# Reordering the first attention layer of a two-layer cross-attention kernel: scores, projection, maxima and a small sum change places

## Chip, cores and metric

The kernel runs on one core of one Trainium2 chip, in one launch. The metric is the device time in microseconds (us); a lower one is better. A profile, where one is shown, is of one execution. Engines are named as in the profile: PE is TensorE (matmuls and transposes), PEld its weight loads, DVE is VectorE, ACT is ScalarE, POOL is GpSimd, SP is SyncE, which here only issues transfers.

## What is computed

There are 32 samples, each with 256 tokens of 256 features, of `x` and of a context. All is in fp32. Two layers follow each other; the reference, cut to what matters:

```python
def L0(tgt, memory, Wq, Wk, Wv):          # 16 heads of 16 features
    q, k, v = heads(tgt @ Wq.T), heads(memory @ Wk.T), heads(memory @ Wv.T)
    probs = softmax(einsum('bhqd,bhkd->bhqk', q, k) / sqrt(16))
    att = merge(einsum('bhqk,bhkd->bhqd', probs, v))
    return tgt + att[0]                    # sample 0's attention is added to every sample

def L1(ctx, x):
    norm_X, norm_F = layernorm(ctx, n1w, n1b), layernorm(x, n2w, n2b)
    attended = softmax(norm_F @ norm_X.T / sqrt(256)) @ norm_X
    h = gelu(attended @ fc1_w.T + fc1_b)   # 4 hidden features
    cross = h @ fc2_w.T + fc2_b
    norm_c = layernorm(cross, n3w, n3b)
    self_att = softmax(norm_c @ norm_c.T / sqrt(256)) @ norm_c
    return norm_F + g2 * (cross + g1 * self_att)

x = L0(x, ctx); x = L1(ctx, x)
```

Only `att[0]` is used, so layer 0 (L0) needs the attention of sample 0 alone. Its result, `att`, is added to each sample of `x`; after that every sample goes through layer 1.

## The kernel before

**L0.** The 16 heads are worked in four "fours", j = 0 to 3. For each four the same steps follow each other, on different engines:

- `head_queries(j)`: PE computes four heads' scores with a row for each query (tiles `sq`, one PSUM bank for a head), eight matmuls of 32 rows (`pair_products`, L445).
- `head_maxima(j, sq, heads)`: DVE takes each query's largest score, negated, into `m_all` (L486), one instruction for a head.
- `head_less(j)`: PE transposes these maxima (`pm`, L493), and DVE adds them to the queries (`qmT`, L498), so that the next scores come out with the maximum already taken off. What it returns is the DVE step; `head_less(j)()` does both at once.
- `head_keys(j)`: PE computes the scores again, with a row for each key (tiles `sk`), and ACT takes their exponentials (`eT_h`, L507), one instruction for a head.
- `head_values(j, copy, by_pairs)`: PE sums exponentials times values (`ph`, L357, eight matmuls), and `copy` brings the result out of PSUM (`col_h`, L368), on ACT or DVE. With `by_pairs` the first two heads' matmuls stand ahead of the others'.
- `head_turned(j)`: PE transposes that (`pt_h`, L375). What it returns, called `weighted`, is DVE's division and its write into `att` (L527, L528).

Between these steps stands work for layer 1: statistics of the context (`stats(n)`, DVE, two instructions L211 for a sample), their moments for four samples (`moments_c` on POOL, L222 to L236, of which L227 is a power; `moments_ahead` on DVE but for the power), the context's normalization (`even_normed` on POOL, L316; `odd_normed` on ACT, L322), and the preparation of small constants (`setup_bias`: PE sums `b1f` into `p_b1f`, L579, and DVE adds a row to make `fc1b_all`, L582; `setup_outer`, `setup_gram`). `project_values(1)` makes the second half of the values `v1` (`pp_v`, L430; copied by ACT, L437).

**After L0.** DVE adds `att` to the first samples (`add_first`, L828) and takes their statistics; POOL makes `rs_x` from them (L227, `first_moments`). For later samples POOL issues transfers that add `att` in memory, four samples each (`add_attention`, L751). Layer 1 then runs one sample a step (`first_step`): normalized `x` is transposed (`turn_x`), scores (`cross_scores`, L779), softmax, transposes and sums. The second attention, over six features, and the output follow in an order written out by hand.

**What sets the order.** Nothing is rescheduled: `tc.manual_schedule()` keeps every engine's instructions in the order in which the program text issues them. An instruction waits, with all behind it on its engine, for the semaphores of those it depends on. [...] The scores rotate over six of them (`four_banks`: `h0` to `h3` and two called `et`). The two others have the tag `tp` and are shared by `pp_v`, `pm`, `ph`, `pt_h`, `p_b1f` and the transposes: the next such tile takes the bank of an earlier one, and its first matmul waits until that one's last reader is done.

Of the kernel before, what the change touches and what calls it, by code (L numbers as in the profile page):

```python
# [22 lines left out]
QB = 4  # L23
# [4 lines left out]
def tile_xattn_seq(  # L28
# [51 lines left out]
    def bank(tag, name):  # L80
        return ps.tile([P, NC, D], F32, tag=tag, name=name)
# [131 lines left out]
    def moments(st, n, name, eng=None):  # L213

        eng = eng or nc.gpsimd

        def t(what, c=1, bufs=2):
            return small.tile([P, n, c], F32, tag=f"{what}{n}", name=f"{what}_{name}", bufs=bufs)

        sm, df, sq, v4, ve, nm = t("sm", 2), t("df"), t("sq"), t("v4"), t("ve"), t("nmean")  # L220
        rs, nmr = t("rs", 1, 3), t("nmr", 1, 3)
        eng.tensor_sub(df, st[:, :, 1:2], st[:, :, 4:5])  # L222
        eng.tensor_add(sm, st[:, :, 1:3], st[:, :, 4:6])
        eng.tensor_mul(sq, df, df)
        eng.tensor_scalar(v4, sm[:, :, 1:2], 4.0 / D, 4 * EPS, ALU.mult, ALU.add)
        eng.tensor_add(ve, v4, sq)
        nc.gpsimd.tensor_tensor(  # L227
            rs.rearrange("p n o -> p (n o)"),
            ve.rearrange("p n o -> p (n o)"),
            neg_half[:, 0:n],  # L230
            ALU.pow,
        )

        def product():
            eng.tensor_scalar(nm, sm[:, :, 0:1], -0.5, 0.0, ALU.mult, ALU.add)
            eng.tensor_mul(nmr, nm, rs)  # L236

        if eng is nc.gpsimd:
            product()
            return rs, nmr  # L240
        return rs, nmr, product
# [11 lines left out]
    def stats_c(n):  # L253
        q, b = n // QB, n % QB
        statistics(st_tile(q - 1)[:, 0, b], cq_of[q][:, b])
# [5 lines left out]
    def flat(st):  # L261
        return st.rearrange("p b t c -> p (b t) c")

    def moments_c(q):
        rn = moments(flat(st_of[q - 1][:, 0]), TQ, f"c{q}")
        for b in range(QB):
            mc_of[q * QB + b] = *rn, b * NC
# [44 lines left out]
    def even_normed(*ns):  # L312
        for n in ns:
            rs, nmr, i = mc_of[n]
            row = cq_of[n // QB][:, n % QB, 0, :]
            nc.gpsimd.tensor_scalar(row, row, rs[:, i, :], nmr[:, i, :], ALU.mult, ALU.add)  # L316

    def odd_normed(*ns):
        for n in ns:
            rs, nmr, i = mc_of[n]  # L320
            row = cq_of[n // QB][:, n % QB, 1, :]
            nc.scalar.activation(  # L322
                row, row, AF.Identity, bias=nmr[:, i + 1, :], scale=rs[:, i + 1, :]
            )
# [22 lines left out]
    def by_columns(psum, name, weights, moving, copy=nc.vector.tensor_copy, by_pairs=False):  # L347
        return copy_columns(columns(psum, name, weights, moving, by_pairs), name, copy)
# [22 lines left out]
    def tokens_first(psum, src, name):  # L371

        pt = psum(f"pt_{name}")
        for t in range(NC):
            nc.tensor.transpose(pt[:, 0, t * P : (t + 1) * P], src[:, t * P : (t + 1) * P], ident)  # L375
        return pt[:, 0, :].rearrange("p (t b c) -> p t b c", t=NC, c=SL)
# [50 lines left out]
    def project_values(t, copy):  # L427
        pp = bank("tp", f"pp_v{t}")
        for dc in range(NC):
            nc.tensor.matmul(  # L430
                pp[:, t, :],
                c0T[:, dc, t * P : (t + 1) * P],
                wvT[:, dc, :],
                start=(dc == 0),
                stop=(dc == NC - 1),
            )
        copy(v1[:, t, :, 0:DK], pp[:, t, :].rearrange("p (h e) -> p h e", e=DK))  # L437

    def pair_products(*pairs):

        for t in range(NC):
            for p, lhs, rhs, dst in pairs:
                for i in range(2):
                    r = SL * (p % 2 * 2 + i)
                    nc.tensor.matmul(  # L445
                        dst[i][:, t, :],
                        lhs[r : r + SL, t * P : (t + 1) * P],
                        rhs[r : r + SL, :],
                        start=True,
                        stop=True,  # L450
                    )
# [4 lines left out]
    def four_banks(name):  # L456

        at = head_banks[0]
        head_banks[0] = (at + QB) % 6
        return [  # L460
            ps0.tile([P, NC, D], F32, tag=f"h{i}", name=f"{name}_{i}")
            if i < QB
            else bank("et", f"{name}_{i}")
            for i in ((at + n) % 6 for n in range(QB))
        ]
# [8 lines left out]
    def head_of(j, i):  # L474
        return 8 * (j // 2) + 2 * i + j % 2

    def head_queries(j):

        sq = four_banks(f"sq{j}")
        qk = qT[:, j, :], kT[:, j, :]  # L480
        pair_products((0, *qk, sq[0:2]), (1, *qk, sq[2:4]))
        return sq

    def head_maxima(j, sq, heads):
        for i in heads:
            nc.vector.tensor_reduce(  # L486
                m_all[:, j % 2, :, i, ones_at[j % 2]], sq[i], AX.X, ALU.max, negate=True
            )

    def head_less(j):  # L490
        pm = bank("tp", f"pm_{j}")
        for t in range(NC):
            nc.tensor.transpose(  # L493
                pm[:, 0, t * P : (t + 1) * P],
                m_all[:, j % 2, t].rearrange("p b c -> p (b c)"),
                ident,
            )
        return lambda: nc.vector.tensor_add(qmT[:, j % 2, :], pm[:, 0, :], qT[:, j, :])  # L498

    def head_keys(j):  # L500

        sk = four_banks(f"sk{j}")
        kq = kT[:, j, :], qmT[:, j % 2, :]
        pair_products((0, *kq, sk[0:2]), (1, *kq, sk[2:4]))
        eT_of[j] = wk.tile([P, QB, NC, D], F32, tag="eTq", name=f"eT_h{j}", bufs=2)
        for i in range(QB):
            nc.scalar.activation(eT_of[j][:, i], sk[i], AF.Exp)  # L507
# [4 lines left out]
    def head_values(j, copy=nc.scalar.copy, by_pairs=False):  # L512
        col_of[j] = by_columns(
            tp_bank,
            f"h{j}",
            lambda kt, i: v1[:, kt, head_of(j, i), :],
            eT_of.pop(j),
            copy,
            by_pairs,
        )  # L520

    def head_turned(j):
        pa = tokens_first(tp_bank, col_of.pop(j), f"h{j}")

        def weighted():
            rd = small.tile([P, NC, QB, 1], F32, tag="rdh", name=f"rd_h{j}")
            nc.vector.reciprocal(rd, pa[:, :, :, DK : DK + 1])  # L527
            nc.vector.tensor_mul(  # L528
                att.rearrange("p t (k i e d) -> p t k i e d", i=QB, e=2, d=DK)[
                    :, :, j // 2, :, j % 2, :  # L530
                ],
                pa[:, :, :, 0:DK],
                rd.to_broadcast([P, NC, QB, DK]),
            )

        return weighted
# [39 lines left out]
    def setup_bias():  # L576
        pb = bank("tp", "p_b1f")
        for dc in range(NC):
            nc.tensor.matmul(  # L579
                pb[:, 0, 0:FH], ones, b1f[:, dc, :], start=(dc == 0), stop=(dc == NC - 1)  # L580
            )
        nc.vector.tensor_add(fc1b_all, pb[:, 0, 0:FH], fc1b_bc)  # L582
# [78 lines left out]
    on_scalar = nc.scalar.copy  # L661

    by_vector = nc.vector.tensor_copy

    def stats(*ns):
        for n in ns:
            stats_c(n)
# [6 lines left out]
    sq = head_queries(0)  # L674
# [5 lines left out]
    sq = head_queries(1)  # L680
# [9 lines left out]
    head_less(1)()  # L690
    setup_outer()
    stats(3)
    project_values(1, on_scalar)
    moments_c(0)
    even_normed(0, 1, 2, 3)
    sq = head_queries(2)
    stats(4)
    head_maxima(2, sq, (0, 1))
    head_values(0)
    setup_bias()  # L700
    head_maxima(2, sq, (2, 3))
    head_keys(1)
    odd_normed(0, 1)
    weighted = head_turned(0)
    stats(5)
    head_less(2)()
    weighted()
    sq = head_queries(3)
    stats(6)
    head_maxima(3, sq, range(QB))  # L710
    head_values(1)
    odd_normed(2, 3)
    head_keys(2)
    weighted = head_turned(1)
    stats(7)
    moments_c(1)
    even_normed(4, 5)
    head_less(3)()
    weighted()
    head_keys(3)  # L720
    stats(8, 9, 10)
    head_values(2, by_vector)
    stats(11)
    odd_normed(4)
    head_values(3, on_scalar, True)
    c_ends = moments_ahead(2)
    weighted = head_turned(2), head_turned(3)
    for f in weighted:
# [632 lines left out]
```

## Time and profile before

| | |
|---|---|
| median of 3 runs | 230.23 us (229.31, 230.23, 233.49) |
| profiled execution | 233.63 us, of which the span from first to last instruction is 231.9 us |
| PE busy | 214.7 us, 93% of the span |
| DVE busy | 169.8 us, 73% |
| POOL busy | 174.8 us, 75% |
| ACT busy | 146.8 us, 63% |
| HBM | 17.73 MB read, 8.39 MB written |
| end of L0 (`att` complete) | 34.85 us from the span's start |

The page gives each engine's busy share, the chain of work that ended last (followed back from the last instruction, at each step to what released it), and groups of instructions by source line. A line of the timeline reads: start, duration, engine, source line, operation, output, input, shape, count, and in brackets how long the engine stood idle before it and what ended that. Times inside the span are counted from its start. The profiled execution is longer than the median; a sum made from its durations belongs to its own time.

### The profile page before, as it was taken

How to read it: one execution, taken by the hardware profiler on the slowest of the kernel's cores; microseconds unless marked ns; L12 is line 12 of the kernel's file. 1: busy time of each engine (PE TensorE's matmuls, PEld its weight loads, DVE VectorE, ACT ScalarE, POOL GpSimd, SP SyncE). 2: the span in 40 equal slices, each digit the busy share in tenths (PEclk: the TensorE clock that was granted, in tenths of full speed). 3: DMA queues.
4: the chain of work that ended last, by engine and by line, in shares of the span. 5: the costliest groups of instructions: out<-in, count | busy, mean ns of one | idle time of the engine just before them, and what ended most of it. 6: DMA issues, size and time to landing. Idle time of an engine off the chain costs nothing.

```text
span 231.9 us, 4950 instructions
## 1 busy us (share of the span) xinstructions
PE 214.7 (93%) x1797; PEld 155.8 (67%) x1797; DVE 169.8 (73%) x409; ACT 146.8 (63%) x299; POOL 174.8 (75%) x276
## 2 busy tenths in 40 slices
PE   7999898898999989999999999989989999999960
PEld 6766556576787768697897887866665666566540
DVE  1797989899988748667686686766384866588791
ACT  2544978698988285966789967456846753444410
POOL 6057598576989999999979999995189999993000
PEclk9999999999999999999999999999999995699996
DMA  6789997999959964180720000000000130444477
GB/s 212 271 310 371 394 383 148 194 256 236 207 104 335 275 117 170 34 151 2 133 51 1 3 0 0 3 4 4 4 0 3 51 133 0 181 184 181 185 281 264
DMA packets 18038, 33.81 MB, mean 146 GB/s; under 512 B 1175, under 2 KB 2142, under 8 KB 18014
## 3 DMA queue, kind: packets, MB, share of 16 engines
q1 hardware_dynamic: 12974, 24.33, 29.3%
q0 software_dynamic: 3696, 7.34, 18.1%
q10 hardware_dynamic: 1344, 1.84, 2.3%
q8 instruction: 14, 0.23, 0.4%
q14 instruction: 10, 0.08, 0.1%
HBM read 17.73 MB, written 8.39 MB: 113 GB/s over the span
## 4 chain that ended last, share of the span: by engine, by line
PE 53%; POOL 23%; DVE 14%; ACT 5%; issue 2%; DVEq 0%; POOLq 0%; ACTq 0%
PE sc L779 13%; POOL x_all L770 5%; PE k L445 4%; PE pt_x L202 4%; PE o L445 3%; PE pt_c L202 3%; POOL cq L307 3%; DVE st L211 3%; PE pt_e L202 3%; PE pu L357 3%; POOL rs_b L227 3%; PE sc L445 2%; POOL rs_x L227 2%; PE ph L357 2%; PE pf L357 2%
## 5 line engine op out<-in xcount | busy, mean ns | idle before, releaser
L779 PE MATMUL sc<-nxT,nfT 128*128 128x256 f32 x256 | 62.4, 386 | 0.7 <-ACT nfT L761 0.7
L779 PEld LDWEIGHTS sc<-nxT,nfT 128*128 128x128 f32 x256 | 45.7, 190 | 12.1 <-issue 5.3
L770 POOL TENSOR_TENSOR x_all<-x_all,w_bc 128x512 f32<-128x512 f32 x32 | 39.8, 1273 | 0.0
L792 ACT ACTIVATE e<-sc,nm 128x256 f32<-128x256 f32 x64 | 26.9, 473 | 19.0 <-DVE nm L789 18.8
L789 DVE TENSOR_REDUCE nm<-sc 128x2 f32<-128x512 f32 x32 | 22.0, 688 | 22.9 <-PE sc L779 11.1
L761 ACT ACTIVATE nfT<-pt_x,bq,wq 128x256 f32<-128x256 f32 x64 | 33.3, 583 | 1.6 <-PE pt_x L202 1.5
L1214 DVE TENSOR_TENSOR x_all<-o,x_all 128x512 f32<-128x512 f32 (+1 forms) x22 | 19.4, 927 | 8.0 <-PE o L445 8.0
L211 DVE BATCH_NORM_STATS2 st<-x_all 128x6 f32<-128x256 f32 x64 | 23.2, 411 | 0.6 <-DMA x_all<-att 0.5
L1209 ACT ACTIVATE eT<-k 128x1024 f32<-128x1024 f32 (+1 forms) x16 | 14.2, 916 | 13.2 <-PE k L445 10.5
L202 PE MATMUL pt_x<-ident,x_all 128*128 128x128 f32 x132 | 20.8, 280 | 1.5 <-POOL x_all L329 1.3
L202 PE MATMUL pt_c<-ident,cq 128*128 128x128 f32 x132 | 19.7, 276 | 1.5 <-ACT nfT L761 1.0
L202 PE MATMUL pt_e<-ident,e 128*128 128x128 f32 x128 | 19.5, 275 | 1.3 <-ACT eTq L801 0.7
L211 DVE BATCH_NORM_STATS2 st<-cq 128x6 f32<-128x256 f32 x56 | 20.6, 412 | 0.0
L307 POOL TENSOR_SCALAR cq<-cq,rs_b,nmr_b 128x256 f32<-128x256 f32 x32 | 19.4, 680 | 0.0
L202 PEld LDWEIGHTS pt_e<-ident,e 128*128 128x128 f32 x128 | 15.4, 141 | 5.0 <-ACT e L792 1.6
L202 PEld LDWEIGHTS pt_x<-ident,x_all 128*128 128x128 f32 x132 | 15.5, 143 | 4.7 <-POOL x_all L329 2.4
L801 ACT COPY eTq<-pt_e 128x512 f32<-128x512 f32 x32 | 18.4, 588 | 0.3 <-PE pt_e L202 0.3
L345 DVE COPY nxT<-pt_c 128x512 f32<-128x512 f32 x23 | 15.6, 677 | 2.3 <-PE pt_c L202 2.3
L202 PEld LDWEIGHTS pt_c<-ident,cq 128*128 128x128 f32 x132 | 15.0, 141 | 3.1 <-ACT nfT L761 1.9
L331 ACT ACTIVATE x_all<-x_all,nmr_b,rs_b 128x256 f32<-128x256 f32 x16 | 9.8, 618 | 10.9 <-POOL nmr_b L236 10.9
L445 PE MATMUL o<-w_out,vt 32*128 32x256 f32 x128 | 15.0, 448 | 0.6 <-ACT vt L1088 0.5
L445 PE MATMUL k<-tt,ut 32*128 32x256 f32 x112 | 15.3, 441 | 0.1
(222 smaller groups left out, 443.8 us busy)
## 6 DMA issues: line engine op xcount, KB each, us to landing
out_dram<-x_all SPq DMA_DIRECT2D x16, 512.0 KB
x_all<-att POOLq DMA_DIRECT2D x7, 1024.0 KB, 9.3
cq<-in_ctx_dram SPq DMA_DIRECT2D x6, 1024.0 KB
x_all<-in_x_dram SPq DMA_DIRECT2D x4, 1024.0 KB
x_all<-in_x_dram SPq DMA_DIRECT2D x1, 2048.0 KB
x_all<-in_x_dram SPq DMA_DIRECT2D x1, 1792.0 KB
cq<-in_ctx_dram ACTq DMA_DIRECT2D x1, 1024.0 KB
cq<-in_ctx_dram SPq DMA_DIRECT2D x1, 768.0 KB
```

The source lines that it names most:

```text
L202: nc.tensor.transpose(pt[:, dc, t * P : (t + 1) * P], src[:, t, dc * P : (dc + 1) * P], ident)
L211: nc.vector.bn_stats(st[:, t, :], src[:, t, :])
L307: nc.gpsimd.tensor_scalar(row, row, rs[:, i + t, :], nmr[:, i + t, :], ALU.mult, ALU.add)
L357: nc.tensor.matmul(pg[SL * b : SL * (b + 1), 0, :], weights(kc, b), moving[:, b, kc, :], start=(kc == 0), stop=(kc == NC - 1),)
L445: nc.tensor.matmul(dst[i][:, t, :], lhs[r : r + SL, t * P : (t + 1) * P], rhs[r : r + SL, :], start=True, stop=True,)
L761: nc.scalar.activation(nfT_of[n][:, dc, :], px[:, dc, :], AF.Identity, bias=bq[:, dc : dc + 1], scale=wq2[:, dc : dc + 1],)
L770: nc.gpsimd.tensor_mul(x_all[:, n], x_all[:, n], w2_bc.unsqueeze(1).to_broadcast([P, NC, D]))
L779: nc.tensor.matmul(sc[:, qt, :], nfT[:, dc, qt * P : (qt + 1) * P], nxT[:, dc, :], start=(dc == 0), stop=(dc == NC - 1),)
L789: nc.vector.tensor_reduce(nm, sc, AX.X, ALU.max, negate=True)
L792: nc.scalar.activation(e[:, qt, :], sc[:, qt, :], AF.Exp, bias=nm[:, qt : qt + 1])
L801: nc.scalar.copy(eT_of[q][:, b], turned(e_of.pop(n), "et", f"e_{n}"))
L1214: nc.vector.tensor_add(xs, po, xs)
```

## The change

Only the order of L0's steps from the third statistics on is changed, all by the text of the program; no operation is added or taken away.

- `head_queries(2)` and `stats(4)` go ahead of `project_values(1)`, and the third four's maxima are taken in one piece, where two and two stood around `head_values(0)` and `setup_bias()`.
- `head_keys(1)` and `head_less(2)` go ahead of `head_values(0)`, and `head_queries(3)` comes between `head_values(0)` and `head_turned(0)`.
- `head_less(3)` goes ahead of the first four's `weighted`, of `stats(6)`, `head_turned(1)` and `stats(7)`; before, `stats(6)` stood ahead of the fourth maxima, and `stats(7)` ahead of `head_less(3)`.
- `head_values(2)` is copied by ACT instead of DVE, and stands ahead of `stats(8, 9, 10)`.
- `setup_bias()` goes from between the third maxima to between `head_values(2)` and `head_values(3)`, behind `stats(8, 9, 10)`.
- `odd_normed(4)` comes behind `head_values(3)`.

```diff
     stats(3)
+    sq = head_queries(2)
+    stats(4)
     project_values(1, on_scalar)
     moments_c(0)
     even_normed(0, 1, 2, 3)
-    sq = head_queries(2)
-    stats(4)
-    head_maxima(2, sq, (0, 1))
+    head_maxima(2, sq, range(QB))
+    head_keys(1)
+    head_less(2)()
     head_values(0)
-    setup_bias()
-    head_maxima(2, sq, (2, 3))
-    head_keys(1)
+    stats(5)
+    sq = head_queries(3)
     odd_normed(0, 1)
     weighted = head_turned(0)
-    stats(5)
-    head_less(2)()
-    weighted()
-    sq = head_queries(3)
-    stats(6)
     head_maxima(3, sq, range(QB))
     head_values(1)
     odd_normed(2, 3)
     head_keys(2)
+    head_less(3)()
+    weighted()
+    stats(6)
     weighted = head_turned(1)
+    head_keys(3)
     stats(7)
+    weighted()
     moments_c(1)
     even_normed(4, 5)
-    head_less(3)()
-    weighted()
-    head_keys(3)
+    head_values(2)
     stats(8, 9, 10)
-    head_values(2, by_vector)
+    setup_bias()
+    head_values(3, on_scalar, True)
     stats(11)
     odd_normed(4)
-    head_values(3, on_scalar, True)
     c_ends = moments_ahead(2)
     weighted = head_turned(2), head_turned(3)
```

## The prediction

> **What bounds the kernel now.** I read the chain that ended last first, then the part of it that the edit touches, then DVE and POOL in order of time, because the edit moves work on those two queues. The page says PE is the busiest engine and carries half of the chain; that is an average over stages.
>
> ```profile
> PE 214.7 (93%) x1797; PEld 155.8 (67%) x1797; DVE 169.8 (73%) x409; ACT 146.8 (63%) x299; POOL 174.8 (75%) x276
> PE 53%; POOL 23%; DVE 14%; ACT 5%; issue 2%; DVEq 0%; POOLq 0%; ACTq 0%
> ```
>
> In order of time the chain runs PE and DVE in turn through L0 (to 34.9 us), then DVE with short POOL steps (to about 64), POOL alone (64 to 93), PE (from 96 on). Nothing on it waits for a transfer. So whatever L0's end gains or loses at 34.9, and whatever POOL's `rs_x` at 37.13 gains or loses, passes to the end.
>
> ```profile
> 25.45 2.38 DVE m_all L486 x4
> 27.83 0.64 DVE st L211 x2
> 28.51 0.44 DVE qmT L498
> 28.99 1.15 PE sk L445 x16
> 30.14 3.25 PE ph L357 x32
> 33.38 0.38 PE pt_h L375 x2
> 34.89 0.70 DVE x_all L828
> ...
> 36.87 0.17 DVE ve_x L226
> 37.13 0.73 POOL rs_x L227
> ```
>
> The last 3.25 us of PE are `ph2` and `ph3`: `ph3` ends at 33.38, and 1.47 us later (transpose, reciprocal, product for two fours) `att` is complete at 34.85. DVE in order of time, with the idle before:
>
> ```profile
> 18.65 0.73 DVE L211 BATCH_NORM_STATS2 st<-cq 128x6 f32<-128x256 f32 x2
> 20.35 1.29 DVE L486 TENSOR_REDUCE m_all<-sq 128x2 f32<-128x512 f32 x2 [0.97 <-PE sq L445]
> 21.91 0.16 DVE L582 TENSOR_TENSOR fc1b_all<-p_b1f,fc1b_bc 128x4 f32<-128x4 f32 x1 [0.27 <-PE p_b1f L579]
> 29.29 2.04 DVE L211 BATCH_NORM_STATS2 st<-cq 128x6 f32<-128x256 f32 x6
> 33.79 0.21 DVE L527 RECIPROCAL rd_h<-pt_h 128x8 f32<-128x8 f32 x1 [0.61 <-PE pt_h L375]
> ```
>
> From 18.65 to 34.89 DVE is idle for only 0.97 + 0.27 + 0.61 = 1.85 us. L0's end is set by how DVE's fixed sum of work is packed as much as by the scores. POOL, same view:
>
> ```profile
> 28.57 0.21 POOL L222 TENSOR_TENSOR df_c<-st 128x8 f32<-128x8 f32 x1 [2.66 <-DVE st L211]
> 32.01 1.16 POOL L316 TENSOR_SCALAR cq<-cq,rs_c,nmr_c 128x256 f32<-128x256 f32 x2
> 33.26 1.64 POOL L227 TENSOR_TENSOR rs_c<-ve_c,neg_half 128x8 f32<-128x8 f32 x1
> 35.17 1.51 POOL L751 DMA_DIRECT2D x_all<-att  x1 [0.28 <-DVE att L528]
> 37.13 0.72 POOL L227 TENSOR_TENSOR rs_x<-ve_x,neg_half 128x2 f32<-128x2 f32 x1 [0.45 <-DVE ve_x L226]
> ```
>
> POOL starts `df_c` when the second quarter's statistics (`stats(7)`) are ready, and from there to `rs_x` it has only 0.28 + 0.45 us of slack.
>
> [...]
>
> **The change part by part.** All times are of the profiled execution. Consecutive DVE instructions overlap by about 0.08, so I step from start to start.
>
> Third scores by queries ahead of the projection. `pt_mk` leaves PE at 17.95; `sq2` no longer waits for `pp_v1` (18.13 to 19.26) but for the second `exp` of the first four (17.26 + 2 x 0.515 = 18.29), which frees its last bank. It is done near 19.3. The gain is not 1.1: DVE holds `stats(3)` and `stats(4)` until 19.30. The maxima, now four in a row (2.47, as the third row of four took), run 19.30 to 21.78 instead of 20.35 to 23.27: 1.5 earlier. `pp_v1` follows at 19.4 to 20.5; its copy on ACT is ready near 20.9, ahead of its user.
>
> Second scores by keys: behind `pp_v1` and the second maximum (20.58), from 20.55 to 21.75; its four exps 21.8 to 23.85 (before 22.97 to 25.03).
>
> The third four's maxima turned now come here: `pm2` 21.9 to 22.33, `qmT` 22.43 (the offset from the last maximum is 0.65, from 27.83 to 28.51 with `pm3`). Then PE does `ph0` (1.01 as before, 22.33 to 23.34), and only then `sq3`, so the fourth maxima start at 23.34 + 1.17 = 24.5. DVE has `stats(5)` (0.66) and nothing more: it is idle about 1.0 us, after 0.65 before `qmT`. The fourth maxima end at 26.98 (before 27.83): of the 1.5 us, 0.85 are left.
>
> PE meanwhile does `pt_h0`, `ph1` (to 25.9) and `sk2` (25.9 to 27.0). ACT does `col0`, two norms (1.11), `col1` (26.3), two norms (to 27.3) and then `sk2`'s exps, 27.3 to 29.3; before 27.56 to 29.60. `pm3` stands behind `sk2`, which ends just then; `qmT` of the fourth 27.66 to 28.08 (before 28.51 to 28.93); DVE was idle another 0.68, which `stats(7)` filled before. `pt_h1` and `sk3` follow, exps of the fourth 29.75 to 31.8 (before 32.27): 0.45 left.
>
> Now DVE's queue, from 28.08 on. Before, six statistics were left; now ten: `stats(6)` and `stats(7)` come behind `qmT` as well as the first four's `weighted`. From the rows: `weighted` 28.0 (0.2 + 0.29, next start at 28.44), four statistics of 0.33 (1.32) to 29.76, `weighted` of the second 0.44 to 30.2, six statistics 1.97 to 32.17, then the bias's sum `fc1b_all` 32.17 to 32.33. `col_h2` (0.34) goes to ACT. `stats(11)` and the five moments (0.66 + 0.17 x 5, partly overlapped: 1.6 as from 31.58 to 33.18) end at 33.87.
>
> The bias's sum is not free at the end. Tag `tp` has two banks. In the built program `ph2` takes one, `p_b1f` the other, and `ph3` gets `p_b1f`'s bank back, so its first matmul waits for DVE's `fc1b_all` as well as for the exps. Before, `fc1b_all` was an early 0.16 on DVE. `ph3` now starts at 32.4, although its last exp is ready at 31.8. Its first half no longer hides behind the exps: 1.05 us is what the last half alone took (32.33 to 33.38), 1.45 if the halves follow in program order (three rounds of about 0.45 instead of two, plus the end). I take 1.4, since the pairs are issued in order: `ph3` ends at 33.8 (33.45 to 33.9), `att` is complete 1.47 later at 35.27 (34.9 to 35.4): **0.42 later than before** (0.07 to 0.5). Without the bank DVE alone would still hold the end: reciprocals from 33.8, as before at 33.79.
>
> POOL: `stats(7)` ends at 29.84 instead of 28.49, 1.35 later. `df_c` to the second even norm take 4.6 (28.57 to 33.17), so they end at 34.52, and `rs_c` of the third quarter, 33.26 before, now 34.5 to 36.14. Behind it stand the first DMA of `att` and `rs_x` of sample 0. The DMA leaves near 36.15, about 0.95 late. It held POOL 0.85 where work followed at once (37.81 to 38.66), at most 1.51 by its own row: `rs_x` can start at 37.0 to 37.66. By DVE it is due at 37.13 + 0.42 = 37.55. The two meet; together I take 37.58, +0.45. The later DMA costs nothing further: it landed 8.6 after issue, 43.8, and is first read at 48.41, 4.6 later.
>
> ACT: `col2`, `col3` and then both odd norms stand ahead of `nxT`; about 0.2 to 0.6 later at 34.75. The work after it has waits of its own (0.18 for `pt_c`; 1.02 in front of the second `x_all`, whose releaser is DVE): hidden. Unknown between 0 and 0.2, I take 0. SP's queue issues nothing in the moved stretch, and no instruction is added or removed, one copy changing engines.
>
> **Sum.** -1.5 (maxima) + 0.65 (`ph0` and `sq3` in PE's order) + 0.4 (ACT's norms, second scores) + 0.87 (bank of `ph3`, its unhidden half) gives +0.42 at `att`; POOL's queue makes +0.45. The profiled execution of 233.63 (span 231.9) becomes 234.1. The runs' median is 230.23, 3.4 below the profiled one; the shift is in L0 and I add it there: **230.7**.
>
> **Rivals.** (A) Faster: the earlier scores reach the end. If `ph3` hid its first half and DVE packed its ten statistics into the 1.0 and 0.68 it stands idle, `att` would come with the exps, 0.45 to 0.85 earlier, and 1.3 with all idle gone: 229.4 (228.9 to 229.8). For it: exps and `qmT` do come earlier. Against: the statistics stand behind `qmT` in DVE's order, and POOL would still hold `rs_x` until 37.0. (B) Slower: POOL decides. It does from where the even norms end after 34.5 and the DMA holds POOL its full 1.51: norms ended at 34.9 give `rs_x` 34.9 + 1.64 + 0.05 + 1.51 = 38.1, +1.0: 231.2 (to 232). For it: POOL's slack of 0.73 against 1.35 of lateness. Against: the 0.85 after the second DMA. (C) The shifts cancel and nothing changes: 230.2.
>
> **How the numbers follow.** Forecast (+0.1 to +0.8) 0.52; A 0.2; B 0.18; C 0.1. The range takes A's middle and B's end and the spread of runs of one kernel (229.31 to 233.49, whose upper value I leave out): 229.2 to 232.2. What a measurement can tell from no change is about 2%, 4.6 us; no case comes near it: faster 0.01, within 0.97, slower 0.02.
>
> **What would show it.** After: four maxima from 19.3, idle of DVE near 1.0 ahead of the fourth maxima; `fc1b_all` near 32.2 and `ph3` released by it; `df_c` near 29.9; `x_all` (the first add) at 35.3; `rs_x` near 37.6. Wrong if `ph3` is released by ACT, if the first add starts before 34.6, or if the later stages differ by more than L0's end does.

## The result and the profile after

The changed kernel takes 229.99 us (median of 22 runs, 229.41 to 231.43), the kernel before, run beside it on the same chip, 229.66 us. The ratio is 1.004, 95% interval 1.0024 to 1.0056: slower by 0.4%, which is 0.9 us. Five of the 22 executions of the kernel before ran near 233.5 us, as did its profiled one (233.63 us), in which PE's granted clock was 0.50 of full speed from 191 to 200 us, long after L0; so the ratio is taken over the other executions, the two medians lie only 0.33 us apart, and spans of two profiles are not subtracted here. The loss is small, but the whole interval lies above 1. The forecast was +0.45 us at 230.7. Single stages are compared, each counted from the start of the second four's `qmT` (before 17.65, after 17.00 us), the last instruction ahead of the edit's effects. The changed program is one line shorter in L0, so L827 and L750 of after are L828 and L751 of before.

First the chain of after that ended last, by engine, from its page:

```profile
PE 41%; POOL 26%; DVE 11%; ACT 7%; issue 3%; DVEq 0%; POOLq 0%; ACTq 0%
```

The shares of the two pages, 53% and 41% for PE, can't be set side by side: the chain of after is followed back only to 19.92 us. What changed is seen in the chain of after, in order of time (start, length, what), at the stretch where L0 ends:

```profile
33.69 1.63 POOL rs_c L227
35.32 1.41 POOL x_all L750
36.73 0.77 POOL rs_x L227
...
37.53 0.41 DVE nmr_x L236
...
37.97 0.95 DVE x_all L329
```

Before, this stretch read PE `sk`, PE `ph`, PE `pt_h`, DVE `x_all`, and POOL came in only with `rs_x`. Now the chain leaves L0's heads after the fourth four's `qmT` (26.91), goes over four of DVE's statistics, and from 29.16 on is POOL's own queue: the second quarter's moments, `rs_c`, the issue of the first transfer (`x_all` L750) and `rs_x`. The last sums of the heads are not on it. DVE of after in order of time (start, length, and in brackets the idle time before it and what ended it), the lines that answer to those of before:

```profile
23.77 2.49 DVE L486 TENSOR_REDUCE m_all<-sq 128x2 f32<-128x512 f32 x4 [0.92 <-PE sq L445]
31.40 0.14 DVE L582 TENSOR_TENSOR fc1b_all<-p_b1f,fc1b_bc 128x4 f32<-128x4 f32 x1
34.37 0.69 DVE L827 TENSOR_TENSOR x_all<-x_all,att 128x512 f32<-128x512 f32 x1
37.53 0.41 DVE L236 TENSOR_TENSOR nmr_x<-nmean_x,rs_x 128x2 f32<-128x2 f32 x1 [0.34 <-POOL rs_x L227]
37.97 0.95 DVE L329 TENSOR_SCALAR x_all<-x_all,rs_x,nmr_x 128x256 f32<-128x256 f32 x1
38.84 0.67 DVE L827 TENSOR_TENSOR x_all<-x_all,att 128x512 f32<-128x512 f32 x1
```

Counted from `qmT`, the first add (the end of L0) starts at 17.37, before at 34.89 - 17.65 = 17.24: only 0.13 later. But the add of sample 1 starts at 21.84, before at 38.66 - 17.65 = 21.01: 0.83 later. The same two instructions of before, not shown yet, in the same view:

```profile
37.88 0.16 DVE L236 TENSOR_TENSOR nmr_x<-nmean_x,rs_x 128x2 f32<-128x2 f32 x1 [0.17 <-POOL rs_x L227]
38.08 0.66 DVE L329 TENSOR_SCALAR x_all<-x_all,rs_x,nmr_x 128x256 f32<-128x256 f32 x1
```

So the 0.83 splits up: `rs_x` ends 0.29 later (37.49 - 17.00 = 20.49 against 37.85 - 17.65 = 20.20), `nmr_x` takes 0.41 for 0.16 (+0.25), and DVE's `x_all` of L329 0.95 for 0.66 (+0.29). From there the shift stays: at 94 us, deep in the second layer, DVE's maximum `nm` starts at 94.77 (before 94.58), which is 0.84 later on the same count. That is the measured 0.9 us. The last view here is POOL of after:

```profile
29.16 0.21 POOL L222 TENSOR_TENSOR df_c<-st 128x8 f32<-128x8 f32 x1 [3.91 <-DVE st L211]
35.27 1.46 POOL L750 DMA_DIRECT2D x_all<-att  x1
36.60 0.89 POOL L227 TENSOR_TENSOR rs_x<-ve_x,neg_half 128x2 f32<-128x2 f32 x1
37.29 1.51 POOL L750 DMA_DIRECT2D x_all<-att  x1
38.13 2.30 POOL L316 TENSOR_SCALAR cq<-cq,rs_c,nmr_c 128x256 f32<-128x256 f32 x2
```

From 29.16 to the end of these POOL has no idle time; before, it waited 0.28 ahead of the first transfer and 0.45 ahead of `rs_x`. The two normalisations L316 behind the second transfer take 2.30 together, before 1.64.

That POOL's queue, and not DVE's `ve_x`, sets the end of `rs_x` is seen over several kernels. `rs_x` is recorded as starting 0.08 to 0.10 after `ve_x` ends in every profile of this document, whether POOL was idle or not. But where POOL came straight from the first transfer's issue, `rs_x` ends 0.75 to 0.77 after the end of the issue's record (in after 35.27 + 1.46 + 0.76 = 37.49), while its own record is 0.77 to 0.96 long; where POOL was idle, it takes 0.70 to 0.72.

### The profile page after: what moved, and what is told of

The parts are those of the page before. It is cut to its first block, busy times and chain, and to the rows that moved or that the text cites. A ratio compares the mean times of both kernels' runs of the same rounds, so it can differ in the third digit from the quotient of the medians.

```text
span 228.1 us, 4956 instructions
## 1 busy us (share of the span) xinstructions
PE 208.2 (91%) x1797; PEld 151.9 (67%) x1797; DVE 170.1 (75%) x408; ACT 147.0 (64%) x300; POOL 175.5 (77%) x276
## 3 DMA queue, kind: packets, MB, share of 16 engines
HBM read 17.73 MB, written 8.39 MB: 115 GB/s over the span
## 4 chain that ended last, share of the span: by engine, by line
PE 41%; POOL 26%; DVE 11%; ACT 7%; issue 3%; DVEq 0%; POOLq 0%; ACTq 0%
PE sc L778 12%; POOL x_all L769 5%; POOL cq L307 3%; PE k L445 3%; PE pt_c L202 3%; PE pt_x L202 3%; PE o L445 3%; PE pt_e L202 3%; DVE st L211 3%; POOL rs_b L227 3%; PE pu L357 2%; POOL rs_c L227 2%; POOL rs_x L227 2%; PE sc L445 2%; PE pv L357 2%
## 5 line engine op out<-in xcount | busy, mean ns | idle before, releaser
L445 PE MATMUL o<-w_out,vt 32*128 32x256 f32 x128 | 13.9, 401 | 0.6 <-ACT vt L1087 0.5
L445 PE MATMUL k<-tt,ut 32*128 32x256 f32 x112 | 13.1, 399 | 0.2
```

Of the source, the lines that this page charges most:

```text
L445: nc.tensor.matmul(dst[i][:, t, :], lhs[r : r + SL, t * P : (t + 1) * P], rhs[r : r + SL, :], start=True, stop=True,)
```

## Theory and rivals

**Theory.** The earlier scores don't reach the end of L0, because DVE's statistics were moved behind the maxima and pack worse. `stats(7)` comes late, so POOL's moments, normalisations, `rs_c`, first transfer and `rs_x` come late. **Rival 1:** the sum for the bias at L0's end, whose PSUM bank `ph3` (the sums of the fourth four) then needs, is the cost. **Rival 2:** the order of the transfers, not the lateness, stretches `rs_x`, `nmr_x` and L329. **Rival 3:** the earlier scores themselves cost or gain.

All readings in one table, in us from the start of the second four's `qmT`. "First add" is the end of L0, "rs_x end" POOL's `rs_x` of sample 0, "add 1" the add of sample 1, and "late" DVE's `nm` near 94 us; a ratio is to the kernel before, run beside it; each of the other columns is read from one profile. The kernel without the first transfer can't be read in this stage and is not in the table (see there).

| kernel | ratio, 95% interval | first add | rs_x end | nmr_x | L329 | add 1 | late |
|---|---|---|---|---|---|---|---|
| before | 1 | 17.24 | 20.20 | 0.16 | 0.66 | 21.01 | 76.93 |
| after | 1.004 (1.0024 to 1.0056) | 17.37 | 20.49 | 0.41 | 0.95 | 21.84 | 77.77 |
| statistics back | 0.9992 (0.9973 to 1.0011) | 16.71 | 19.66 | 0.16 | 0.67 | 20.48 | 76.31 |
| bias early | 1.0037 (1.0022 to 1.0052) | 17.12 | 20.51 | 0.33 | 1.02 | 21.85 | 77.67 |
| transfers moved | 1.005 (1.0022 to 1.0078) | 17.38 | 20.30 | 0.16 | 0.83 | 21.28 | 77.70 |
| before, statistics late | 1.0049 (1.0031 to 1.0068) | 17.78 | 20.79 | 0.16 | 0.68 | 21.63 | 77.56 |
| the same, ACT freed | 1.0053 (1.0036 to 1.007) | 17.24 | 20.78 | 0.33 | 1.02 | 22.12 | 77.95 |
| scores alone | 1.0004 (0.9983 to 1.0026) | 17.30 | 20.25 | 0.16 | 0.66 | 21.07 | 76.87 |
| statistics and bias | 0.998 (0.9967 to 0.9994) | 16.95 | 19.96 | 0.16 | 0.68 | 20.79 | 76.72 |
| L316 behind | 1.004 (1.0021 to 1.0058) | 17.37 | 20.48 | 0.16 | 0.68 | 21.31 | - |
| transfer behind L316 | 1.0016 (0.9997 to 1.0034) | 17.37 | 20.48 | 0.53 | 0.61 | 21.62 | 77.44 |

The late shift and the measured ratio agree in sign: +0.51 to +1.02 goes with 1.0016 to 1.0053, -0.21 and -0.62 with 0.998 and 0.9992. Their sizes don't follow each other closely, as these last two show.

## Experiments

### Statistics back

On the kernel after, `stats(5)` goes between the third four's transposed maxima and their add, and `stats(6, 7)` ahead of the fourth maxima, into the two places where DVE stood idle:

```diff
-    head_less(2)()
+    less = head_less(2)
+    stats(5)
+    less()
     head_values(0)
-    stats(5)
     sq = head_queries(3)
...
     weighted = head_turned(0)
+    stats(6, 7)
     head_maxima(3, sq, range(QB))
...
-    stats(6)
...
-    stats(7)
```

> The kernel after, with stats(5) ahead of the third qmT and stats(6), stats(7) ahead of the fourth maxima, where DVE stood idle 0.65 and 0.92 us. Packing theory (DVE's fixed sum sets L0's end, and POOL's queue waits for stats(7)): the earlier scores now reach the end, att about 0.75 us earlier than after, df_c on POOL near 23.8 instead of 29.2, the x_all of sample 0 on DVE back at 0.66 us; in all 1.2 to 1.5 us faster than after, that is 0.995 to 0.998 of the kernel before. Rival, the bank of ph3 alone holds the end: fc1b_all moves up with DVE's queue here too, so the same sign, but rs_x, nmr_x and x_all stay long and the gain ends at 0.75: 1.000 to 1.001. Rival, the order of PE (ph0 and sq3 behind pm2) holds it: no gain over after, 1.004.

Measured: 229.0 us, ratio 0.9992; by the two ratios, about 1.1 us are won against the kernel after (1.2 to 1.5 expected). DVE of this kernel in order of time, then POOL:

```profile
24.48 2.49 DVE L486 TENSOR_REDUCE m_all<-sq 128x2 f32<-128x512 f32 x4 [0.26 <-PE sq L445]
33.26 0.21 DVE L527 RECIPROCAL rd_h<-pt_h 128x8 f32<-128x8 f32 x1 [0.48 <-PE pt_h L375]
```

```profile
36.65 0.71 POOL L227 TENSOR_TENSOR rs_x<-ve_x,neg_half 128x2 f32<-128x2 f32 x1 [0.45 <-DVE ve_x L226]
```

The idle time ahead of the third four's `qmT` is gone and that ahead of the fourth maxima fell from 0.92 to 0.26. DVE has its statistics done in time: it waits again for PE at the first of the last two reciprocals, and L0 ends 0.66 earlier than in the kernel after (0.53 earlier than before). POOL waits 2.44 for DVE, and `rs_x` waits 0.45 for `ve_x` as it did before. `nmr_x` and L329 are back at 0.16 and 0.67. So what the change lost hangs on where the statistics stand, the rest of the change is worth some 0.5 us in the trace once DVE is packed, and the time followed in sign: it is no longer measurably slower than before, and the gain over before that the trace shows (0.53 us, 0.2%) lies just inside the interval.

### Bias early

On the kernel after, `setup_bias()` stands ahead of `head_values(2)`:

```diff
     even_normed(4, 5)
+    setup_bias()
     head_values(2)
     stats(8, 9, 10)
-    setup_bias()
```

> The kernel after, with only setup_bias() moved ahead of head_values(2), so that fc1b_all stands ahead of the last eight statistics and ph3's bank is free early. Bank theory: ph3 is released by its exponentials, its first half hides again, L0 ends 0.6 to 0.75 us earlier than after: 1.001 of before. Packing theory: DVE still reaches the last reciprocals at 33.2 (it had no idle time there in after), att at most 0.17 us earlier, and POOL, which holds rs_x until 36.6, not at all: 1.003 to 1.004, as after, with ph3's end near 32.0 instead of 32.8.

Measured: 1.0037, no gain. The first add comes 0.25 sooner (17.12 for 17.37), so rival 1 is right that the bank delays L0's heads. But `rs_x` ends at 20.51, as in the kernel after (20.49): the first transfer's issue starts at the same point (18.28 for 18.27 after `qmT`), and `rs_x` ends 0.76 after its record does. So L0's end doesn't set `rs_x` in these two kernels. DVE kept only 0.05 of the 0.25 up to `ve_x` as well: its `v_x`, beside the issue, took 0.36 for 0.17.

### Transfers moved

On the kernel after, each accumulating transfer is issued behind a later POOL step: the first behind `rs_x` of sample 0, the second behind `ends()` of samples 1.

```diff
-    add_attention(QB, 2 * QB)
     add_first(0)
     ends = first_moments(0, 1)
+    add_attention(QB, 2 * QB)
...
-    add_attention(2 * QB, 3 * QB)
...
     ends()
+    add_attention(2 * QB, 3 * QB)
```

> The kernel after, with POOL's first add_attention moved behind rs_x of sample 0 and its second behind the first x_all of POOL; L0 untouched. Queue theory (rs_x runs back to back behind a transfer's issue, and what it and the next DVE steps lose comes from the two issues so close together): rs_x starts near 36.6 as in after, since ve_x is ready only at 36.5, but takes 0.7 instead of 0.89, nmr_x 0.16 instead of 0.41 and x_all 0.66 instead of 0.95; about 0.7 us faster than after, 1.001 of before. Rival, any issue that follows rs_x stretches the two DVE steps beside it: they stay at 0.4 and 0.95, no gain, 1.004. Rival, the loss lies in L0 itself: no gain, 1.004.

Measured: 1.005, no gain. With no transfer ahead of it `rs_x` takes 0.70 and ends 0.19 sooner than in the kernel after, `nmr_x` 0.16, and the add of sample 1 comes 0.56 sooner. Then it is given back at the second transfer's new place, issued at 42.61, as DVE shows there:

```profile
42.98 0.44 DVE L225 TENSOR_SCALAR v_x<-sm_x 128x2 f32<-128x2 f32 x1
43.53 0.40 DVE L235 TENSOR_SCALAR nmean_c<-sm_c 128x8 f32<-128x8 f32 x1
```

DVE's small `v_x` and `nmean_c`, 0.17 each in the kernel after, take 0.44 and 0.40 here, and `rs_x` 0.99 for 0.70. No L316 stands near: the last had ended at 40.14. The late shift is +0.77, nearly that of the kernel after. Neither place for the issue was free of cost. Rival 2 is right in part: `nmr_x` went back to 0.16, L329 only to 0.83.

### Before, statistics late

The lateness alone, on the kernel before: `stats(7)`, `moments_c(1)` and `even_normed(4, 5)` behind the third four's sums and the fourth scores by keys.

```diff
     weighted = head_turned(1)
-    stats(7)
-    moments_c(1)
-    even_normed(4, 5)
     head_less(3)()
     weighted()
     head_keys(3)
+    stats(7)
+    moments_c(1)
+    even_normed(4, 5)
     stats(8, 9, 10)
```

> The kernel before, with only stats(7), its moments and even norms moved behind head_keys(3). DVE then idles some 0.6 us ahead of the fourth qmT and has the two statistics later. Queue theory: L0 ends within 0.1 us of before, but POOL's df_c comes 1.4 us later, the first transfer leaves near 36.2 and rs_x near 37.6: 0.45 us from the start of rs_x alone, 0.7 to 1.2 with longer rs_x, nmr_x and x_all: 1.002 to 1.005 of before, so most of what the whole change costs. Rival, POOL's slack covers it and the whole change's cost comes from DVE's packing or the bank: 1.000 (0.999 to 1.001).

Measured: 1.0049, as much as the whole change costs. But not on the expected path: the end of L0 came 0.54 later, where I had expected at most 0.1. ACT in order of time shows why:

```profile
33.64 0.60 ACT L322 ACTIVATE cq<-cq,nmr_c,rs_c 128x256 f32<-128x256 f32 x1 [1.20 <-POOL nmr_c L236]
34.14 0.35 ACT L368 COPY col_h<-ph 128x256 f32<-128x256 f32 x1
```

ACT's normalisation `odd_normed(4)` waits 1.20 for POOL's late `nmr_c`, and the fourth four's copy `col_h` stands behind it; the fourth reciprocal on DVE then waits 0.54 for its transpose. So L0's end was delayed by way of ACT. Whether that was also what delayed `rs_x` (ended at 20.79, +0.59) this run can't tell; the next one frees ACT.

### The same, ACT freed

The kernel of the last experiment with `odd_normed(4)` behind `head_values(3)`:

```diff
-    odd_normed(4)
     head_values(3, on_scalar, True)
+    odd_normed(4)
```

> The kernel before with stats(7), moments_c(1) and even_normed(4, 5) behind third four's sums and fourth four's scores (as in the late-stats run), and with odd_normed(4) moved behind head_values(3), so that ACT's copies of the heads no longer stand behind a normalisation that waits for POOL. Theory: the end of L0 is back within 0.15 us of the kernel before, POOL is as late as in the late-stats run (first issue 0.8 to 1.0 us late, no idle time ahead of rs_x), and it costs only where POOL's lateness reaches rs_x: first step 0.1 to 0.5 us late, ratio 1.000 to 1.003. Rival: POOL's lateness alone makes up the whole loss of the changed kernel: ratio 1.003 to 1.006 with the end of L0 unchanged.

Measured: 1.0053, the rival's value. The end of L0 is back at 17.24, exactly that of before, yet `rs_x` ends at 20.78, as in the last experiment and 0.58 later than before, and `nmr_x` and L329 are stretched, as DVE in order of time has them:

```profile
38.68 0.33 DVE L236 TENSOR_TENSOR nmr_x<-nmean_x,rs_x 128x2 f32<-128x2 f32 x1 [0.41 <-POOL rs_x L227]
39.05 1.02 DVE L329 TENSOR_SCALAR x_all<-x_all,rs_x,nmr_x 128x256 f32<-128x256 f32 x1
```

So the detour over ACT did not set `rs_x` there; POOL's queue did in both. The add of sample 1 is 1.11 later, of which 0.58 is POOL's lateness and 0.53 the two stretched DVE instructions. A third one is stretched here, ahead of `rs_x`:

```profile
36.90 0.51 DVE L225 TENSOR_SCALAR v_x<-sm_x 128x2 f32<-128x2 f32 x1
```

It ran beside the first transfer's issue (36.42 to 37.88), after the L316 before that had ended at 34.88. So POOL's lateness alone, with L0's end where it was, makes a loss of the size of the change's. I had priced it at 0.1 to 0.5.

### Scores alone

On the kernel before, only the first part of the change: third four's scores and `stats(4)` ahead of the projection, maxima uncut, `setup_bias()` behind them.

```diff
+    sq = head_queries(2)
+    stats(4)
     project_values(1, on_scalar)
     moments_c(0)
     even_normed(0, 1, 2, 3)
-    sq = head_queries(2)
-    stats(4)
-    head_maxima(2, sq, (0, 1))
+    head_maxima(2, sq, range(QB))
     head_values(0)
     setup_bias()
-    head_maxima(2, sq, (2, 3))
     head_keys(1)
```

> One part alone on the kernel before: third four's scores by queries and stats(4) ahead of the projection of the second keys, their maxima uncut behind even_normed, and setup_bias behind the maxima; the rest as before. Theory: DVE has nothing else to do at that place, third four's maxima begin some 0.5 us sooner, but the end of L0 is set by fourth four, whose DVE queue is unchanged in sum: ratio 0.998 to 1.001, end of L0 within 0.3 us of the kernel before. Rival (earlier scores reach the end): the end of L0 comes 0.4 to 1.3 us sooner and the ratio is 0.994 to 0.998.

Measured: 1.0004, end of L0 +0.06, everything else as before. The earlier maxima by themselves neither gain nor cost within the interval. They are not handed on, though: the third four's `qmT` waits 0.90 and starts 6.33 after the second's, before 6.27, in the kernel after 4.77. So rival 3 falls for this first part only; what the earlier `qmT` is worth is seen in statistics back.

### Statistics and bias

Both repairs on the kernel after (statistics back, and `setup_bias()` ahead of `head_values(2)`):

> Both repairs together on the kernel after: stats(5) between third four's totals and their sum, stats(6, 7) ahead of fourth four's maxima, and setup_bias ahead of head_values(2). Theory: with the stats early POOL is out of the way (rs_c of the second group done before the last att sum), so that the end of L0 is set by fourth four's heads again, and fc1b_all no longer holds their scores' bank; that bank is then released by third four's exps 0.3 to 0.4 us sooner. Expected: att 0.2 to 0.5 us earlier than with the stats alone (aligned on second four's qmT), ratio to the kernel before 0.995 to 0.998. Rival: fourth four's rd_h or the ACT copies between set the end anyway, and it stays with the stats alone at 0.998 to 1.000.

Measured: 228.74 us, 0.998 (0.9967 to 0.9994): the one version here whose interval lies below 1, by 0.2%. The expected mechanism was wrong, though. With the statistics alone `ph3` is done at 32.85 - 17.70 = 15.15, here at 32.88 - 17.73 = 15.15: the bank held nothing up. There `ph3` had waited 0.35 for `fc1b_all` and yet ended no later; the last exponentials, which end at 14.04 and 14.03, fit as what sets its end. And `fc1b_all` now waits on DVE ahead of eight statistics:

```profile
30.20 0.16 DVE L582 TENSOR_TENSOR fc1b_all<-p_b1f,fc1b_bc 128x4 f32<-128x4 f32 x1 [1.08 <-PE p_b1f L579]
```

It costs 0.24 at the first add (16.95 for 16.71). The trace thus puts this kernel behind the one with the statistics alone, and the times put it ahead of that one by less than the two intervals can tell apart. Which of them is better stays open.

### No first transfer

This is the kernel after without `add_attention(QB, 2 * QB)`, which leaves samples 4 to 7 without `att`.

> The kernel after, without the transfer that adds att to samples 4 to 7 (so these samples lack att; all work on them is otherwise done). Theory: in the kernel after, POOL issues two accumulating transfers only 2.02 us apart, with rs_x between them and no idle time, and that stretches rs_x (0.89 for 0.72), nmr_x (0.41 for 0.16) and DVE's x_all of L329 (0.95 for 0.66). With one of the two gone these three go back to 0.70 to 0.72, 0.16 and 0.66 to 0.68, and the first step is 0.6 to 0.75 us earlier: ratio to the kernel before 0.999 to 1.002. Rival: the stretching comes from the second transfer and its neighbours alone (the transfer itself beside them, or the normalisations behind it on POOL): then nmr_x and L329 stay at 0.4 and 0.95, only rs_x shortens, and the ratio stays at 1.003 to 1.005.

> The kernel without the first transfer a second time (samples 4 to 7 lack att), because the clock of PE was down to 0.5 in its profile just in the stage that is asked about. With the clock at full speed there: rs_x is released by DVE's ve_x, takes 0.70, the remaining transfer begins within 0.12 us of nmr_x's start, nmr_x takes 0.16 and L329 0.66; sample 1's add is then 0.7 to 0.9 us earlier than in the kernel after. If the time is again 1.003 to 1.006 of the kernel before, then that gain isn't what decides the time, or the missing transfer costs elsewhere.

Measured: 1.0038 (1.002 to 1.0057) and 1.0036 (1.0011 to 1.0061): no gain where 0.6 to 0.75 us had been expected. Both profiles have PE's granted clock at 0.50 of full speed from 35 to 37 us, where the kernel after has 1.00; the windows of the second (stretch, length, busy PE, PEld, DVE, ACT, POOL, then PE's clock, DMA share, GB/s):

```profile
35.00:37.00 2.00, 2.00 (x12) 2.00 (x11) 1.75 (x5) 1.20 (x4) 1.40 (x1) 0.50 0.38 141
```

DVE waits 1.21 for PE's slowed transposes, so the stage can't be read for the question, and why the time didn't fall is not settled. One thing can be read: the only transfer of the stage was issued at 38.59, 1.75 before `nmr_x`, and still `nmr_x` took 0.42 and `nmean_x` 0.56, both beside POOL's L316 (39.65 to 41.21). That pointed to L316.

### L316 behind, and transfer behind L316

Two more edits of the kernel after look for what stretches `nmr_x` and L329. My guess tried in both is that the two take longer where POOL's L316 runs beside them; in the first edit also that a transfer's issue beside `nmr_x` does the same. In the first, `even_normed(6, 7)` (L316) goes behind `rs_x` of samples 1; in the second, it goes directly behind `rs_x` of sample 0, and the transfer behind it.

```diff
     add_attention(2 * QB, 3 * QB)
-    even_normed(6, 7)
     add_first(1)
     ends = first_moments(1, 2)
+    even_normed(6, 7)
```

> The kernel after with even_normed(6, 7), POOL's normalisations that follow its second transfer, moved behind the statistics of sample 1 (behind rs_x of samples 1). Theory [...]: nmr_x starts 0.24 us into the issue as before and still takes 0.33 to 0.41; L329's x_all no longer has POOL's L316 beside it; if that collision is what stretches it, it takes 0.66 to 0.70 again and sample 1's add is 0.25 to 0.3 us earlier; the rest of the gain can be lost where L316 now stands ahead of POOL's x_all of sample 1: ratio 1.001 to 1.006. Rival (the issue alone stretches both): L329 stays at 0.95 with no L316 beside it.

```diff
-    add_attention(2 * QB, 3 * QB)
     even_normed(6, 7)
+    add_attention(2 * QB, 3 * QB)
     add_first(1)
```

> The kernel after with POOL's second transfer moved behind even_normed(6, 7), so that the normalisations L316 and not the issue follow rs_x of sample 0. Theory [...]: L316 starts with rs_x's end, ahead of nmr_x[...]: nmr_x 0.4 to 0.6[...]. Sample 1's add between 0.3 us earlier and 0.3 us later than in the kernel after, ratio 1.002 to 1.006. Rival (only the issue of a transfer stretches DVE): nmr_x 0.16 and L329 0.66, sample 1's add 0.5 us earlier, ratio 1.001 to 1.003.

Measured, L316 behind: 1.004. The transfer is where it was (0.22 us ahead of `nmr_x`), and both stretches are gone; the new neighbour of L316, `nmr_x` of sample 1, got one. DVE, then POOL:

```profile
37.62 0.16 DVE L236 TENSOR_TENSOR nmr_x<-nmean_x,rs_x 128x2 f32<-128x2 f32 x1 [0.32 <-POOL rs_x L227]
37.82 0.68 DVE L329 TENSOR_SCALAR x_all<-x_all,rs_x,nmr_x 128x256 f32<-128x256 f32 x1
41.77 0.53 DVE L236 TENSOR_TENSOR nmr_x<-nmean_x,rs_x 128x2 f32<-128x2 f32 x1 [0.54 <-POOL rs_x L227]
```

```profile
41.75 1.08 POOL L316 TENSOR_SCALAR cq<-cq,rs_c,nmr_c 128x256 f32<-128x256 f32 x2
```

My expectation that the issue would still stretch `nmr_x` was wrong. With the issue at nearly the same place as in the kernel after (0.24 us ahead of `nmr_x` there), both stretches went with L316. The add of sample 1 comes 0.53 sooner than in the kernel after, and the gain is lost again, since L316 now stands ahead of POOL's own `x_all` of sample 1 (42.83 - 17.11 = 25.72, in the kernel after 25.46). PE slowed down near 46 us in this profile (four `sc` matmuls from 44.74 took 1.67, in the kernel after seven from 44.38 took 1.80; the mean granted clock was 0.98), so its late reading is left out.

Measured, transfer behind L316: 1.0016. L316 starts 0.19 ahead of `nmr_x`, which takes 0.53 (POOL, then DVE):

```profile
37.31 1.22 POOL L316 TENSOR_SCALAR cq<-cq,rs_c,nmr_c 128x256 f32<-128x256 f32 x2
```

```profile
37.50 0.53 DVE L236 TENSOR_TENSOR nmr_x<-nmean_x,rs_x 128x2 f32<-128x2 f32 x1 [0.33 <-POOL rs_x L227]
```

The rival, by which only an issue stretches DVE, is refuted. The add of sample 1 is 0.22 sooner than in the kernel after; POOL finishes L316 early, in 1.22 for 2.30.

## Why the prediction came out as it did

**Right: DVE's packing.** On the prediction's clock (0.65 added to the times of after) the third maxima run 19.30 to 21.77 (predicted 19.30 to 21.78), the fourth start at 24.42 (24.5) after 0.92 idle (1.0), the fourth `qmT` at 27.56 (27.66) and `fc1b_all` at 32.05 (32.17). The earlier scores came, and the ten statistics behind `qmT` ate them. Statistics back shows that this was the cause, and that half of rival A's condition, packing the statistics into the idle time, does bring L0's end forward, by 0.53.

**Right in kind, too large in size: the bank of `ph3`.** It is released by `fc1b_all` as foretold, at 32.33 (32.4). PE of after:

```profile
31.68 1.09 PE L357 MATMUL ph<-eT_h,v 128*32 128x256 f32 x16 [1.25 <-DVE fc1b_all L582]
```

But it took 1.09, near the lower bound of 1.05, where I chose 1.4, an estimate in which the halves follow each other. All its exponentials were ready, and the whole four took hardly more than its last half had before. With that, L0's end moved by 0.13 and not 0.42; this is the mis-sized term of the sum. Removing the bank's wait (bias early) gained 0.25 at the first add and nothing in time.

**Too small: POOL's share.** The prediction had the queue right: `df_c` at 29.81 (29.9), third quarter's `rs_c` at 34.34 (34.5), the transfer at 35.92 (36.15). The choice was the issue's hold on POOL: 0.85 to 1.51, taken so that DVE and POOL met and POOL added 0.03. On the chain it held POOL for 1.41, and POOL set the end of `rs_x`: 0.29 later, where L0's end by itself would have made 0.13. So POOL added 0.16. That is the mechanism of rival B at a smaller size. B's own sum, with the norms ended at 34.36 as they did, gives 34.36 + 1.64 + 0.05 + 1.51 = 37.56, which is +0.43; the measured steps, `rs_c` from 34.34 for 1.63 and the issue for 1.41, give 37.38, which is +0.25.

**Not foreseen: POOL's work against DVE's.** 0.54 of the 0.83, the larger part, comes from `nmr_x` and L329, which I had carried over with their old durations. Started beside L316, `nmr_x` took 0.53 in both of the last two kernels (0.02 and 0.19 behind L316's start), and with L316 moved away 0.16. POOL's two L316 differ too: in the kernel before they took 1.64 from 38.66, where DVE's L329 (38.08 to 38.74) was running as they started, and 1.16 from 32.01 in L0. In three kernels one thing stays open: in after, bias early, and the same with ACT freed, `nmr_x` (0.41, 0.33, 0.33) had ended 0.19 to 0.21 before L316 is recorded as started, with only the second issue on record beside it. And `v_x` took 0.36, 0.51 and 0.44 beside an issue, 2.0 or more after the last L316 had ended, while in after and the last two kernels it took 0.16 beside one. Why a few tenths of lateness bring the stretch on is not shown. In after, bias early, and the same with ACT freed, the first transfer still held POOL when `rs_x` was recorded as started (`rs_x` 0.89 to 0.96 long), and the second transfer began 0.20 to 0.28 ahead of `rs_x`'s end instead of 0.02 to 0.09. The kernel with L316 behind has nearly the same (0.87 and 0.19), and no stretch of `nmr_x` and L329.

Taken together the predicted sign was right and the size was half of what came: +0.45 against +0.84 in the trace, just above the forecast's own +0.1 to +0.8 and below rival B's +1.0. A measurement could also tell more than the prediction thought: not 2%, but some 0.16% to either side. Of the +0.45, 0.42 had been laid to L0's heads, where 0.13 came. That the time still fell near the forecast owes something to luck: an oversized term at the heads was made up by one that was missing. The prediction had named its sign for this, later stages that differ by more than L0's end does, and it came true: 0.83 at the add of sample 1 against 0.13.

## What to carry to other kernels

When instructions are moved on one engine, follow the queue of the engine that consumes their results to its next urgent instruction: here late statistics on DVE left L0's end where it was (17.24 with and without, once ACT was freed) and made POOL late for the step on which everything waits. Statistics and other filler belong into the idle places that a reordering opens, not behind them. And when POOL's work slides, look at which DVE instructions it will now run beside: here two durations from the old profile no longer held (`nmr_x` 0.41 for 0.16, L329 0.95 for 0.66).

## What was not expected of the hardware

- DVE's small product `nmr_x` (128x2), started beside POOL's 128x256 normalisation (L316), took 0.53 us instead of 0.16 in two kernels. With a transfer's issue in between, in three others, `nmr_x` took 0.33 to 0.41 and DVE's 128x256 `tensor_scalar` 0.95 to 1.02 instead of 0.66.
- The issue of an accumulating transfer of 1 MB held POOL for 1.41 us ahead of `rs_x`. Beside such an issue, with no normalisation near, DVE's `v_x` (128x2) took 0.36 to 0.51 us instead of 0.17 in three kernels, but `nmr_x` kept its 0.16 where the issue was 0.22 us old. Which instructions are stretched, and when, these runs don't settle.
